# One gated feed-forward block on one core: conditioning rows through TensorE, three weights turned by transfers, and two roots by GpSimd at the start

## The chip, the cores and the metric

The kernel runs on one core of a Trainium2 chip. The time is that of one execution on the device, in microseconds (us). Five engines work side by side, each in the order of its own instruction list: TensorE (PE, with its weight loads as PEld), VectorE (DVE), ScalarE (ACT), GpSimd (POOL) and SyncE (SP), which here does nothing but issue transfers. One SP queue carries nearly all of them; an issue that has to wait holds everything behind it on SP.

## The reference

x has 4 batches of 1024 tokens with 512 features, `up_w` 4096 rows of 512, `down_w` 512 rows of 2048, and `cond` one row of 128 for each batch.

```python
scale = cond @ norm_w.T + 1.0
ms = jnp.mean(x * x, axis=-1, keepdims=True)
h = x * (scale[:, None, :] * jax.lax.rsqrt(ms + EPS))
u = h @ up_w.T
val, gate = jnp.split(u, 2, axis=-1)
h = val * jax.nn.gelu(gate, approximate=False)
hq = h + jax.lax.stop_gradient(act_quant(h) - h)
wq = down_w + jax.lax.stop_gradient(weight_quant(down_w) - down_w)
y = hq @ wq.T
return y + x
```

`act_quant` rounds each token's h to 8 bits by its largest value, `weight_quant` rounds `down_w` to -1, 0 and 1.

## The kernel before

**Tiles.** A batch's up product is cut into 16 slots (j = 0 to 15). Each slot has the 128 gate rows and the 128 value rows of `up_w` that belong together, and gives 128 hidden features for 1024 tokens. Operands are split into a high and a low float16 part, so a product of two tiles has three terms.

**Batch 0** (`plain`, `plain_half`, `plain_first`) multiplies in the plain way: for each slot, each half of 512 tokens and each of gate and value, 12 matmuls of 128x128 by 512 (L917; L960 for the first of all). The order of halves is (0,0), (1,0), (2,0), (0,1), (1,1), (2,1), then (j,0), (j,1) for j from 3 on; the latter are in `first_batch`. Batches 1 to 3 (`slot`, `product`, L902) use a seven-product scheme with sums of weight blocks, and the down product of an earlier batch runs between.

**Weights on the way to TensorE, in batch 0.** `w_load` brings weight j into one of three places (`wn(j)`, by j modulo 3). `w_range` finds its scale. From there two paths lead to the float16 tile `s_tile(j)`, which is one of three buffers, also by j modulo 3:

- for j below `ROWS` (6): `w_scale` on GpSimd (ScalarE for one tile of weight 1), `w_turn` (8 turns on TensorE through PSUM, L646), `w_high` and `w_low` (float16 parts out of PSUM, ScalarE and VectorE), and `w_evac` (a float32 copy `wf(j)` for the sums);
- for j from `ROWS` on: `w_scale` on ScalarE, then `w_rows`: the float16 parts are made untransposed in a staging slot, H[15 + j % 2], and one SP transfer turns them into parts 3 to 6 of `s_tile(j)` (L662). `wf(0)` and `wf(1)` lie in the same two staging slots, 15 and 16.

In both, `s_sums` (GpSimd), `s_high` (ScalarE) and `s_low` (GpSimd) form the sums that the later batches need, in one scratch tile `sf`, and `s_spill` writes the tile to DRAM: one transfer of 896 KB below `ROWS`, three transfers above it, since sums of such a weight are kept unturned. `s_load` brings tiles back in batches 1 to 3, turning the unturned parts on the way. A buffer of `s_tile` can only be filled anew when its products have run and its spill has landed.

**Conditioning.** `cond_first_row` and `cond_scale` make batch 0's scale at the start; `cond_scale_rest` makes the other three in `scT` (128 partitions by 4 blocks by 4 batches). `cond_range`, `cond_spread` and `cond_undo` find powers of two per batch. `cond_rows` writes `scT` for batches 1 to 3 to DRAM as rows (L567: three transfers of 512 pieces of four bytes), in `first_batch(3)`; `cond_load_scale` reads one row back, spread over all partitions (L572, at j = 5 for batch 1), and `cond_bring` scales it on VectorE (L576).

**The start.** x's first four tiles of 128 tokens arrive two by two. ScalarE squares and sums them (L1238), one square root on ScalarE with a refining step on VectorE (`rsqrt_start`) gives all four factors, the tiles are scaled (VectorE, GpSimd and ScalarE), turned on TensorE (`first_turn`, L1262), and turned into float16 (`first_high`, `first_low`, L1266 and L1270). `keep_warm` issues products of zeros. PSUM tiles are handed out in rings by tag: "A" and "E" have two banks, "po" three, "B" one, and the next tile of a tag takes the next bank of its ring, waiting for its last reader.

**Order.** Every call on an engine is recorded as a step by `Plan.add` with an estimated cost. `order` places and replays the steps 40 times with chance variations and emits the best order found, so the program text doesn't fix the order on an engine, except that the first `HEAD` (150) steps, transfers aside, keep program order on their engine. `price` puts four-byte pieces of a transfer at 1.5 KB a microsecond.

Of the kernel before, what the change touches and what calls it, by code (L numbers as in the profile page):

```python
# [114 lines left out]
class Plan:  # L115


    def __init__(self):
        self.steps = []
        self.wrote, self.read = {}, {}  # L120
        self.loaded, self.last = {}, {}
        self.lines = {}

# [4 lines left out]
    def add(self, eng, method, real, args, kwargs):  # L128
# [88 lines left out]
    def place(self, margin, guard):  # L217

        steps = self.steps
        used = {e: Line() for e in ("PE", "ACT", "DVE", "POOL", "SP", "DMA")}
        for s in sorted(steps, key=lambda s: (s.late, s.n)):
            t = max((steps[d].end + lag(steps[d], s) for d in s.deps), default=0.0)
            if s.eng != "PE":
                t += min(margin, max(0.0, s.late - t) * 0.1)
            if s.wait > 0.1:
                t = used["DMA"].put(t + ISSUE, s.wait) - ISSUE
            near = 0.0 if s.eng == "PE" or s.late - t > 1.0 else guard  # L230
            s.start = used[s.eng].put(t - s.before, s.before + s.cost, near) + s.before
            s.end = s.start + (ISSUE + s.wait + LANDING if s.wait else s.cost)
# [39 lines left out]
HEAD = 150  # L272
MARGINS = ((0.3, 0.0), (0.3, 0.15), (0.3, 0.3), (0.25, 0.1))
ROUNDS, MISSES, ISSUE, LANDING, RELOAD = 40, 6, 1.2, 1.5, 6.5
# [106 lines left out]
def glu_quant_kernel(  # L381
# [64 lines left out]
    rows_dram = tc.dram_tile([B, D], F32, name="rows_dram")  # L446
# [105 lines left out]
    def cond_spread(dg, b0, b1, tag):  # L552
        n = b1 - b0
        pd = bank(tag, {"po": 3}.get(tag, 2), [P, B], f"pd_{b0}")[:, :n]
        PE.matmul(pd, ones[:n, :], dg, start=True, stop=True)
        return pd
# [7 lines left out]
    def cond_rows():  # L564

        for b in range(1, B):
            SP.dma_start(out=rows_dram[b].rearrange("(k p) -> p k", p=P), in_=scT[:, :, b])  # L567

    def cond_load_scale(b):

        sc = wpool.tile([P, D], F32, name=f"sc_{b}", tag="sc", bufs=1)
        SP.dma_start(out=sc, in_=rows_dram[b].partition_broadcast(P))  # L572
        return sc
# [55 lines left out]
    ROWS = 6  # L629
# [36 lines left out]
    def w_high(j, ts=(1, 0)):  # L666
        gate, a21, a22 = a_parts(j)
        g, v = (p.rearrange("p (n f) -> p n f", n=2) for p in pw[j])
        if 1 in ts:
            ACT.copy(gate[:, :, 0], g)  # L670
        if 0 in ts:
            ACT.copy(a21[:, 0], v[:, 0])
            ACT.copy(a22[:, 0], v[:, 1])
# [547 lines left out]
    ACT.activation(start_t, one, AF.Sqrt)  # L1221
# [19 lines left out]

    def rsqrt_start(t, y):

        z = sm.tile([P, NA], F32, name="newton", bufs=1)
        ACT.activation(z, t, AF.Sqrt, scale=1.0 / D, bias=eps)
        DVE.tensor_scalar(t, t, 1.0 / D, EPS, ALU.mult, ALU.add)
        DVE.reciprocal(y, z)
        DVE.tensor_tensor(z, y, y, ALU.mult)
        DVE.scalar_tensor_tensor(z, z, -0.5, t, ALU.mult, ALU.mult)
        DVE.scalar_tensor_tensor(y, z, 1.5, y, ALU.add, ALU.mult)  # L1250
# [73 lines left out]
    def second_part():  # L1324
# [6 lines left out]
        ACT.activation(start_t, neghalf[:, 0:1], AF.Gelu)  # L1331


# [22 lines left out]
    def first_batch(j, sc):  # L1356

        if j + 2 <= ROWS:
            w_load(j + 4)
# [5 lines left out]
        rows = ROWS <= n < NJ  # L1365
        if j + 1 < ROWS:
            s_sums(j + 1)
        elif rows:
            s_sums(n)
# [5 lines left out]
        if j + 3 < ROWS:  # L1375
            w_scale(j + 3)
        plain_half(j, 0)
        if j == 3:
            pd = cond_spread(dg, 1, B, "po")
            cond_undo(pd, 1, B)  # L1380
            cond_rows()
# [4 lines left out]
        if j + 1 < ROWS:  # L1386
            s_all(j + 1)
        if n < ROWS:
            w_turn(n)
            w_high(n)  # L1390
            w_evac(n)
            w_low(n)
# [9 lines left out]
        if j + 2 > ROWS and j + 5 < NJ:  # L1402
            w_load(j + 5)
# [3 lines left out]
        if odd:  # L1407
            t.turn()
# [3 lines left out]
        own = rows and j + 1 >= ROWS  # L1412
        if own:
            s_high(n)
            s_low(n, POOL)
        if ROWS <= j + 3 < NJ:
            w_scale(j + 3)
            w_rows(j + 3)
        if own:
            s_spill(n)  # L1420
        elif rows:
            s_sums(n)
            s_all(n)
            w_load(j + 5)
# [59 lines left out]
    w_scale(3)  # L1484
# [18 lines left out]
    w_load(6)  # L1503
# [405 lines left out]
```

## Time and profile before

| | |
|---|---|
| median of 3 runs | 745.95 us (745.18 to 746.45) |
| profiled execution | 745.51 us, of which span 743.7 us |
| TensorE (PE) busy | 725.1 us, 97% of the span |
| VectorE (DVE) busy | 595.4 us, 80% |
| ScalarE (ACT) busy | 405.5 us, 55% |
| GpSimd (POOL) busy | 213.0 us, 29% |
| TensorE's granted clock, mean | 0.995 |
| data moved | 115.74 MB, mean 156 GB/s |

In the views below, times count from the start of the span. A row of the timeline has start, duration, engine, line of the kernel, operation, tile written and tile read, how many instructions were merged, and in brackets how long the engine had been idle and what released it. A row of grouped instructions has their total and mean duration. "PEclk" is the clock that TensorE was granted, as a share of full speed. Matmul ends are modelled, so pace is better read from counts over a stretch than from the mean of one.

### The profile page before, as it was taken

What the parts mean: (1) busy time and instruction counts of PE and PEld (TensorE: products, weight loads), DVE (VectorE), ACT (ScalarE), POOL (GpSimd) and SP (SyncE); (2) the same over time, 40 slices, a digit from 0 to 9 for tenths busy, and PEclk for the clock granted to TensorE, in tenths of its full rate; (3) what the DMA queues carried; (4) which work ended last, traced back from release to release, by engine and by line L of the source; (5) the groups of instructions that cost most, each with busy time, mean ns of one, the idle gap of its engine ahead of it and who ended that gap; (6) DMA issues with size and microseconds to landing.
All of it is one profiled execution on the core that took longest, in us unless ns stands there. A gap on an engine that the chain in (4) does not pass through costs nothing.

```text
span 743.7 us, 10243 instructions
## 1 busy us (share of the span) xinstructions
PE 725.1 (97%) x3684; PEld 362.7 (49%) x3684; DVE 595.4 (80%) x816; ACT 405.5 (55%) x675; POOL 213.0 (29%) x213
## 2 busy tenths in 40 slices
PE   7997899999999999999999999999999999999997
PEld 3553344444444445666444445566444444445743
DVE  6984899869788888877588888878668888855997
ACT  5984687768256677523434767623333666332363
POOL 1575788866640004700004104700000000000010
PEclk9998999999999999999999999999999999999999
DMA  6887788999843465687743455596753444443504
GB/s 240 297 221 98 164 238 192 237 257 247 236 120 99 107 155 115 163 189 178 204 123 100 109 133 145 129 207 147 172 151 106 102 104 100 100 99 100 142 30 170
DMA packets 179567, 115.74 MB, mean 156 GB/s; under 512 B 141750, under 2 KB 147767, under 8 KB 179516
## 3 DMA queue, kind: packets, MB, share of 16 engines
q1 hardware_dynamic: 179226, 114.76, 60.9%
q8 instruction: 29, 0.48, 0.3%
q10 hardware_dynamic: 290, 0.33, 0.1%
q14 instruction: 22, 0.18, 0.1%
HBM read 58.93 MB, written 23.09 MB: 110 GB/s over the span
## 4 chain that ended last, share of the span: by engine, by line
PE 91%; DVE 4%; DMA 3%; ACT 1%; issue 1%; SPq 0%; DVEq 0%; ACTq 0%
PE A L902 33%; PE E L902 17%; PE E L917 10%; PE po L1173 8%; PE B L902 8%; PE A L917 6%; PE B L917 5%; DMA s_dram<-SXY 2%; DVE H L1094 2%; DMA H<-in_x_dram 1%; PE A L1122 1%; PE B L1173 0%; PE po L646 0%; DVE am L1063 0%; PE A L960 0%
## 5 line engine op out<-in xcount | busy, mean ns | idle before, releaser
L902 PEld LDWEIGHTS <-SXY 128*128 128x128 f16 x2016 | 197.3, 98 | 227.9
L902 PE MATMUL A<-R,SXY 128*128 128x512 f16 x1152 | 270.1, 379 | 0.0
L902 PE MATMUL E<-R,SXY 128*128 128x512 f16 x576 | 142.9, 379 | 0.0
L1052 POOL PARTITION_ALL_REDUCE am<-R x8 | 15.6, 1946 | 285.5 <-DVE R L1038 285.5
L1094 DVE TENSOR_TENSOR H<-H,am 128x1024 f32<-128x1024 f32 x64 | 78.1, 1249 | 0.1
L917 PEld LDWEIGHTS <-SXY 128*128 128x128 f16 x462 | 45.4, 98 | 54.5 <-issue 0.8
L902 PE MATMUL B<-R,SXY 128*128 128x512 f16 x288 | 70.8, 379 | 0.0
L1036 DVE TENSOR_REDUCE gm<-H 128x512 f32<-128x1024 f32 x56 | 69.0, 1231 | 0.6
L1000 DVE SCALAR_TENSOR_TENSOR H<-A,sg,t 128x512 f32<-128x512 f32 x48 | 36.0, 749 | 39.0 <-PE A L902 38.3
L988 ACT COPY B<-A 128x512 f32<-128x512 f32 x48 | 27.4, 570 | 67.5 <-PE A L902 66.9
L1173 PE MATMUL po<-wd,R 128*128 128x256 fp8e4 (+1 forms) x448 | 59.1, 275 | 0.0
L980 ACT COPY t<-A 128x512 f32<-128x512 f32 x48 | 28.1, 586 | 56.2 <-PE A L902 56.2
L1013 ACT ACTIVATE t<-t,sg 128x512 f32<-128x512 f32 x48 | 34.6, 722 | 38.3 <-DVE t L1010 38.2
L1173 PEld LDWEIGHTS <-R 128*128 128x128 bf16 (+1 forms) x480 | 47.0, 98 | 15.9
L1016 DVE TENSOR_TENSOR v<-A,v 128x512 f32<-128x512 f32 x48 | 33.2, 691 | 25.2 <-PE A L902 24.0
L997 ACT ACTIVATE t<-B,sg 128x512 f32<-128x512 f32 x48 | 33.0, 687 | 34.2 <-PE B L902 33.7
L1010 DVE TENSOR_TENSOR t<-E,t 128x512 f32<-128x512 f32 x48 | 33.1, 689 | 21.0 <-PE E L902 20.6
L917 PE MATMUL E<-R,SXY 128*128 128x512 f16 x210 | 49.7, 379 | 0.0
L917 PE MATMUL E<-R 128*128 128x512 f16 x162 | 39.9, 385 | 7.7 <-DVE H L945 7.7
L917 PEld LDWEIGHTS <-R 128*128 128x128 f16 x282 | 27.7, 99 | 40.2 <-issue 8.6
L1102 ACT ACTIVATE H<-H 128x1024 f32<-128x1024 f32 x38 | 40.0, 1056 | 8.6 <-DVE H L1094 8.6
L1038 DVE TENSOR_TENSOR R<-R,gm 128x512 f32<-128x512 f32 x56 | 42.9, 765 | 0.9
(234 smaller groups left out, 1040.2 us busy)
## 6 DMA issues: line engine op xcount, KB each, us to landing
SXY<-s_dram SPq DMA_DIRECT2D x66, 256.0 KB, 2.7
SXY<-s_dram SPq DMA_DIRECT2D x18, 384.0 KB, 3.4
H<-in_L_cond_up_w_dram SPq DMA_DIRECT2D x13, 512.0 KB, 4.6
s_dram<-SXY SPq DMA_DIRECT2D x14, 384.0 KB, 5.0
xr<-in_x_dram SPq DMA_DIRECT2D x19, 256.0 KB, 3.0
out_dram<-xr SPq DMA_DIRECT2D x19, 256.0 KB, 2.7
H<-in_x_dram SPq DMA_DIRECT2D x8, 512.0 KB, 4.3
R<-in_L_cond_down_w_dram SPq DMA_DIRECT2D x8, 512.0 KB, 5.5
```

The source lines that it names most:

```text
L902: PE.matmul(o, s[:, w, k, :], tv[:, :, c, l, k, :], start=start and n == 0, stop=stop and n == len(TERMS) - 1, skip_group_check=True,)
L917: PE.matmul(ps, a[k // 2][:, w, k % 2, :], XP[:, l, k, h * TOK : (h + 1) * TOK], start=n == 0, stop=n == len(terms) - 1,)
L997: ACT.activation(cur["t1"], pb, AF.Gelu, scale=gain(g, 1))
L1000: DVE.scalar_tensor_tensor(h_half(g - 1, 0), prev["A"], gain(g - 1, 0), prev["t1"], ALU.mult, ALU.mult)
L1010: DVE.tensor_tensor(prev["t2"], prev["E"], prev["t2"], ALU.add)
L1013: ACT.activation(prev["t2"], prev["t2"], AF.Gelu, scale=gain(g - 1, 1))
L1016: DVE.tensor_tensor(cur["v"], cur["A"], cur["v"], ALU.add)
L1036: DVE.tensor_reduce(gm[0], v, AX.X, ALU.max, apply_absolute_value=True)
L1038: return [largest, lambda: DVE.tensor_tensor(m, m, gm[0], ALU.max)]
L1094: DVE.tensor_tensor(v, v, r.to_broadcast([P, 2, TOK]), ALU.mult)
L1102: ACT.activation(v, v, AF.Copy, bias=MAGIC)
L1173: PE.matmul(po, w[:, j], m, start=start and j == 0, stop=stop and j == n - 1, skip_group_check=True,)
```

## The change

The diff has four parts.

- `cond_rows` turns all of `scT` (16 columns) on TensorE into 16 rows, copies them out of PSUM, and writes them by one transfer of 16 rows of 512 bytes; it now runs right behind `cond_largest(1, B)`. `cond_load_scale` reads a row back as four pieces.
- `ROWS` goes from 6 to 3: weights 3, 4 and 5 take the path of `w_rows`. The calls around slots 0 to 2 and `first_batch` are rearranged to suit; `w_load(6)` and `w_load(7)` move behind the sums of weights 3 and 4, which now read the loaded weight itself.
- At the start, `rsqrt_start` goes. Tiles 0 and 1 get their factors by `rsqrt` (GpSimd's power) as soon as their sums are there, tiles 2 and 3 by a second one; VectorE sums tile 3; scaling and turning go in the order 0, 1, 3, 2, with two warming products between. The product of `cond_spread` takes bank B. The table of Gelu is loaded at the start, and the second table load goes.
- In the planner, steps are tied to program order until `book.tied = False` behind the last `first_turn` of the first four tiles, in place of the first 150; and a step that depends on a transfer is placed up to 4 us (`FERRY`) behind its planned end where there is time.

```diff
+        self.tied = True
...
-            if s.n < HEAD and eng in self.last:
+            if self.tied and eng in self.last:
                 deps.add(self.last[eng])
...
+            for d in s.deps:
+                if steps[d].wait:
+                    t = max(t, steps[d].end + min(FERRY, max(0.0, s.late - steps[d].end - 4.0) * 0.3))
...
-    rows_dram = tc.dram_tile([B, D], F32, name="rows_dram")
+    rows_dram = tc.dram_tile([D // P * B, P], F32, name="rows_dram")
...
     def cond_rows():
-        for b in range(1, B):
-            SP.dma_start(out=rows_dram[b].rearrange("(k p) -> p k", p=P), in_=scT[:, :, b])
+        n = NK * B
+        pr, v = po_bank("pr", [n, P]), H[:n, 8, 0, 64 : 64 + P]
+        PE.transpose(pr, scT.rearrange("p k b -> p (k b)"), ident)
+        DVE.tensor_copy(v, pr)
+        SP.dma_start(out=rows_dram, in_=v)
...
-        SP.dma_start(out=sc, in_=rows_dram[b].partition_broadcast(P))
+        v = rows_dram.rearrange("(k b) p -> b k p", b=B)[b].partition_broadcast(P)
+        SP.dma_start(out=sc.rearrange("q (k p) -> q k p", k=NK), in_=v)
...
-    ROWS = 6
+    ROWS = 3
...
-    ACT.activation(start_t, one, AF.Sqrt)
+    ACT.activation(start_t, one, AF.Gelu)
...
-    for n in range(NA):
-        first_sum(n)
     keep_warm(2)
-    pd = cond_spread(cond_range(pm, 0, 1), 0, 1, "A")
-    keep_warm(7)
-    am = w_largest(0, 1, 2)
-    rsqrt_start(ssq0[:, 0:NA], rs0[:, 0:NA])
-    for n, eng in ((3, DVE), (0, ACT), (2, POOL), (1, ACT)):
-        first_scale(n, eng)
-    w_factor(0, am, 1, 2)
+    pd = cond_spread(cond_range(pm, 0, 1), 0, 1, "B")
+    cond_undo(pd, 0, 1)
+    keep_warm(5)
+    first_sum(0)
+    first_sum(1)
+    rsqrt(ssq0[:, 0:2], rs0[:, 0:2])
+    first_sum(2)
+    first_sum(3, DVE)
+    first_scale(0, ACT)
+    first_scale(1, ACT)
+    rsqrt(ssq0[:, 2:4], rs0[:, 2:4])
+    w_range(0, 1, 2)
+    first_scale(3, DVE)
+    first_scale(2, ACT)
     w_scale(0, (1,))
-    cond_undo(pd, 0, 1)
     ptx = [po_bank(f"ptx_0_{k}") for k in range(3)] + [bank("A", 2, name="ptx_0_3")]
-    for n in (3, 0, 2, 1):
-        first_turn(n, ptx)
+    first_turn(0, ptx)
+    first_turn(1, ptx)
+    keep_warm(2)
+    first_turn(3, ptx)
+    first_turn(2, ptx)
+    book.tied = False
...
-        ACT.activation(start_t, neghalf[:, 0:1], AF.Gelu)
...
     mx = cond_largest(1, B)
+    cond_rows()
     plain_half(0, 1)
     w_range(4)
     w_gain(4)
-    w_scale(4)
+    w_scale(3)
+    w_rows(3)
     s_all(1)
     s_sums(2)
-    w_turn(3)
-    w_high(3)
-    w_evac(3)
-    w_low(3)
...
     plain_half(1, 1)
-    w_load(6)
...
-    w_scale(5)
+    w_scale(4)
+    w_rows(4)
     s_all(2)
     s_sums(3)
+    w_load(6)
...
-    w_turn(4)
-    w_high(4)
-    w_evac(4)
-    w_low(4)
     plain_half(2, 1)
+    w_scale(5)
+    w_rows(5)
     s_all(3)
+    s_sums(4)
+    s_all(4)
+    w_load(7)
```

In `first_batch(j)` the calls for turning on TensorE go, and every j now runs, in this order: sums of weight j + 2, range of j + 3, the first half, `w_load(j + 5)`, the second half, `s_all(j + 2)`, `w_scale(j + 3)` and `w_rows(j + 3)`, for as long as there are such weights.

More of the change, by code (lines that the diff above doesn't have):

```diff
@@ L553, in cond_spread @@
         n = b1 - b0
[L554 removed]
+        pd = bank(tag, {"po": 3, "B": 1}.get(tag, 2), [P, B], f"pd_{b0}")[:, :n]
         PE.matmul(pd, ones[:n, :], dg, start=True, stop=True)
@@ L664, in w_rows, with w_high @@
         )
-    def w_high(j, ts=(1, 0)):
+    def w_high(j, ts=(1, 0), copy=ACT.copy):
         gate, a21, a22 = a_parts(j)
@@ L669, in w_high @@
         if 1 in ts:
-            ACT.copy(gate[:, :, 0], g)
+            copy(gate[:, :, 0], g)
         if 0 in ts:
@@ L1411, in first_batch @@
             d_mean(part)
[L1412 to L1416, printed above, removed]
+        if n < NJ:
+            s_all(n)
+        if j + 3 < NJ:
             w_scale(j + 3)
             w_rows(j + 3)
[L1419 to L1424, printed above, removed]
         for m in D_ROUND[j] if j == D_MEAN else ():
```

32 lines of the change are left out of this document (3 added, 29 removed).

## The prediction

> **What bounds the kernel now.** I began with TensorE, which is busy for 97% of the span, and asked in which stretch the other 3% lie. The table of stretches gives busy time per engine, granted clock, DMA share and GB/s.
>
> ```profile
> span 743.7 us, 10243 instructions
> ```
>
> ```profile
> 60.00:65.00 5.00, 4.76 (x24) 2.31 (x23) 1.20 (x2) 3.74 (x7) 4.51 (x6) 1.00 0.16 38
> 65.00:70.00 5.00, 0.21 (x1) 0.10 (x1) 2.51 (x5) 0.00 (x0) 0.90 (x2) 0.84 1.48 268
> 70.00:75.00 5.00, 4.54 (x15) 2.50 (x14) 1.18 (x3) 0.37 (x1) 0.00 (x0) 0.50 1.01 44
> ...
> 90.00:200.20 110.20, 110.20 (x512) 49.92 (x511) 94.29 (x109) 74.88 (x130) 85.10 (x82) 1.00 0.91 225
> 200.20:743.70 543.50, 538.47 (x2809) 274.54 (x2807) 435.06 (x556) 268.48 (x421) 81.32 (x76) 1.00 0.52 133
> ```
>
> From 90 us on TensorE is the bound. Between 65 and 70 us it does nothing, and in the 5 us behind that it runs at half clock. The DMA engines are over 100% busy there and then move only 44 GB/s: many small packets. The list of TensorE's waits names the releaser.
>
> ```profile
> PE E L917 <- DVE H L945: 7.7, 2, 5.0
> ```
>
> VectorE is not the cause, though; it was waiting itself. The timeline gives start, duration, engine and line:
>
> ```profile
> 50.27 0.46 SPq L567 DMA_DIRECT2D rows_dram<-scT  x1
> ...
> 61.80 0.34 SPq L572 DMA_DIRECT2D sc<-rows_dram  x1
> ...
> 62.67 1.52 SPq L567 DMA_DIRECT2D rows_dram<-scT  x2
> ...
> 64.30 1.68 SPq L714 DMA_DIRECT2D s_dram<-SXY  x1
> ...
> 67.46 0.49 DVE L576 TENSOR_SCALAR sc<-sc,ux 128x512 f32<-128x512 f32 x1 [6.26 <-DMA sc<-rows_dram]
> ...
> 69.00 0.74 DVE L945 SCALAR_TENSOR_TENSOR H<-E,sg,t 128x512 f32<-128x512 f32 x1
> ```
>
> The SP queue's waits and the chain of waits complete it:
>
> ```profile
> SPq L572 <- DMA rows_dram<-scT: 9.5, 1, 9.5
> ```
>
> ```profile
> 64.30 17.26 DMA s_dram<-SXY
> ```
>
> The 2 KB row of batch 1, written in pieces of four bytes (L567), has not landed 9.5 us after SP turns to the load that reads it. SP issues nothing meanwhile. Then VectorE stands 6.26 us before L576, with TensorE's evacuation (L945) queued behind it: that is the 5.0 us stop. The other two rows go out at 62.67, and the spill behind them takes 17.26 us; it lands at 81.6, holds a weight buffer till then, and a second stop of 2.7 us (7.7 less 5.0) follows.
>
> **The change, part by part.** (1) *The rows as 16 rows of 512 bytes.* What the stall costs I count in matmuls, by line L917 alone (busy time and count in TensorE's column) and, in the second fence, by the weights' turns (L646):
>
> ```profile
> 60.00:90.00 30.00, 19.95 (x85) 8.64 (x84) 0.89 0.82 156
> 90.00:200.20 110.20, 110.16 (x511) 49.72 (x509) 1.00 0.91 225
> ```
>
> ```profile
> 30.00:60.00 30.00, 2.40 (x16) 2.00 (x16) 1.00 0.79 213
> 60.00:90.00 30.00, 2.18 (x8) 1.71 (x8) 0.89 0.82 156
> ```
>
> ```profile
> 31.11 0.49 PE L1262 MATMUL po<-ident,H 128*128 128x128 f32 x3
> ...
> 32.86 2.75 PE L917 MATMUL E<-R 128*128 128x512 f16 x12
> ```
>
> A matmul takes 110.16/511 = 0.2156 us at full clock, and the 16 turns from 31.11 to 32.86 took 1.75, 0.109 each. The work between 60 and 90 us is then 85 x 0.2156 + 8 x 0.109 = 19.2 of 30 us. 0.1 us went on two small products, so stops and the low clock behind them cost 10.7 us. All of it has its origin in the row writes, and I take **-10.7** for it. Bounds: not below -10.7; at the other end nothing, if another transfer holds the engines. Whether the others could keep up without the stop: VectorE, the fullest of them, has 94.29 us of work in the 110.2 us behind it (86%) and had 1.20 + 2.51 + 1.18 = 4.9 us in the 15 us above, so it has room.
>
> What is put in its place, and moved ahead from slot 3 to just behind the conditioning's products: one turn, one copy of 16 partitions, one SP issue, instead of three issues. On SP it goes past the loads of weights 6 and 7 and the spills of slots 1 and 2, which now wait up to one issue (0.46 us) behind it, and longer if the copy is late. TensorE has one small product more ahead of half (0,1). Its nearest row for landing is another small write:
>
> ```profile
> SPq L1077 <- DMA am_dram<-am: 1.5, 2, 0.8
> ```
>
> A reader of 4 KB waited 0.8 us at most for its writer. Lower bound nothing, upper bound 9.5 us as today; I take the lower row, because its pieces are long too. A load of a row is now in four pieces for each partition; VectorE needs it only some 20 us after the write can have landed, and that covers it. Cost 0; with the cover gone, at most the 6.3 us of L576.
>
> (2) *Weights 3 to 5 by transfers.* The 24 turns go: 24 x 0.109 = **-2.6** on TensorE, which is full there. GpSimd loses its scalings. The rest:
>
> ```profile
> L636 ACT ACTIVATE H<-H,iv 128x512 f32<-128x512 f32 x21 | 13.9, 713 | 7.0 <-DVE iv L619 7.0
> ...
> L661 DVE TENSOR_TENSOR H<-H 128x1024 f16<-128x1024 f32 x10 | 14.7, 1472 | 1.7 <-ACT H L660 1.7
> ...
> L660 ACT CAST H<-H 128x1024 f16<-128x1024 f32 x10 | 10.4, 1045 | 0.5 <-POOL H L697 0.3
> ...
> L686 ACT COPY H<-po 128x512 f32<-128x512 f32 x10 | 5.9, 590 | 0.3 <-DVE SXY L679 0.2
> ...
> L670 ACT CAST SXY<-po 128x512 f16<-128x512 f32 x3 | 1.7, 577 | 0.0
> ```
>
> ```profile
> L662 SPq DMA_TRANSPOSE SXY<-H x7: 1935/2304/3119, 82.1 to 177.9; - x7
> ...
> DMA to landing us min/median/max: 4.3/4.8/5.1
> ```
>
> ```profile
> 40.09 0.72 POOL L695 TENSOR_TENSOR H<-H 128x256 f32<-128x256 f32 x1
> ...
> 52.85 2.75 PE L917 MATMUL B<-R,SXY 128*128 128x512 f16 x12
> ```
>
> ScalarE gains 2 x 0.713 + 1.045 = 2.5 us a weight and loses two copies (1.2), a cast (0.58) and two casts of half the size (0.29 to 0.58 each): 2.3 to 2.9. VectorE swaps three subtractions over 1,024 elements for one (1.47). So both stay where they are. New is a wait: weight 3's float16 copy goes to the staging slot that the sums of weight 1 read until 40.81 (L695). From there copy 1.05, subtraction 1.47, and 4.8 from issue to landing make 48.1; 50.4 if the 2.3 us of issuing come on top. Slot 3 starts at 52.85, less the 16 turns (1.75) 51.1. The cover is thus 0.7 to 3.0 us, thin. Behind the waiting transfer SP holds weight 6's load, due much later. With longest issue and landing and one more pass of ScalarE and VectorE (2.5) it would land at 54.0: 2.9 late, some 4 with the slow clock that followed the old stop. Bounds 0 to +4; I take **+1.0**, since the middle of the estimate is in time. Slots 4 and 5 come 10 and 21 us later. In batches 1 to 3 these three weights' reloads turn too, with 18 issues more on SP; after 200.2 us the DMA share is 0.52 and each tile is fetched a slot (some 9 us) ahead, so 0.
>
> A page of the Trainium skill speaks against this part: VectorE: DVE Perf Modes, "The three transpose paths" and the rules behind it, says to turn 128x128 blocks on TensorE where PSUM will do, and gives 390 ns there against 1309 ns by transfer. A weight has 16 such blocks in float16, so by that page alone an estimate is 20.9 us for a weight, slot 3 would start 43.3 + 20.9 - 51.1 = 13.1 us late, and the sum would be 744.6 (732.5 - 1.0 + 13.1). The trace has 4.8 us for just this transfer; the sum goes by the trace, and that extreme gets 0.01 of the chance of late weights below.
>
> (3) *The start.*
>
> ```profile
> 8.56 0.63 ACT L1238 ACTIVATE R<-H 128x512 f32<-128x512 f32 x1 [0.84 <-DMA H<-in_x_dram]
> ...
> 11.13 1.34 ACT L1255 ACTIVATE H<-H,rs 128x512 f32<-128x512 f32 x2 [0.91 <-DVE rs L1250]
> ...
> 13.91 0.69 ACT L1266 ACTIVATE R<-po,scT 128x512 f16<-128x512 f32 x1 [1.43 <-DVE sw L616]
> ...
> 15.31 0.39 PE L960 MATMUL B<-R,SXY 128*128 128x512 f16 x1 [0.68 <-ACT SXY L670]
> ...
> 18.04 0.60 PE L960 MATMUL A<-R 128*128 128x512 f16 x2
> ...
> 20.52 0.74 DVE L1270 SCALAR_TENSOR_TENSOR R<-A,scT,R 128x512 f16<-128x512 f32 x1
> ...
> 27.81 1.06 POOL L807 TENSOR_TENSOR rs<-ssq,neghalf 128x4 f32<-128x4 f32 x1 [0.84 <-DVE ssq L806]
> ```
>
> ```profile
> 65.07 0.19 POOL L806 TENSOR_SCALAR ssq<-ssq 128x2 f32<-128x2 f32 x1 [0.40 <-ACT xt L836]
> 65.34 0.71 POOL L807 TENSOR_TENSOR rs<-ssq,neghalf 128x2 f32<-128x2 f32 x1
> ```
>
> A root of two tiles takes GpSimd 66.05 - 65.07 = 1.0 us. The first can run while ScalarE squares tile 2 (8.56 to 9.2). ScalarE then scales tiles 0 and 1 (1.34) till about 10.7, when the second root is ready (squares done about 9.5, plus 1.0 and hops); tile 2 follows till 11.4, tile 3 on VectorE beside it. Turning a tile takes 4 x 0.109 = 0.44 us, and with two warming products (2 x 0.216) between, the last ends about 12.4; the first float16 of x starts at 12.4 where it started at 13.91: **-1.5**. Bounds: 0, if the products are fed no sooner, to -2.5. One thing is lost. Counting the tiles of tag A, the value product's bank used to be the other one than that of x's fourth turn; it is now the same, so the first value product must follow its last reader (L1270, 20.52 to 21.26) and not precede it as at 18.04. In today's order that would be 3.2 us; VectorE's steps there are no longer tied to program order, so it can come forward. I take **+0.4** of 0 to 3.2. ScalarE's second table load goes, in a stretch where TensorE runs anyway: 0.
>
> The planner's new spacing behind transfers changes orders everywhere; behind 200 us TensorE loses nothing that it could give back, so 0 within 0.7 either way.
>
> Sum: the profiled execution took 745.51 us, of which 743.7 are span. 745.51 - 10.7 - 2.6 + 1.0 - 1.5 + 0.4 = 732.1. The median of the runs shown is 745.95, 0.44 more: **732.5**.
>
> **The rivals.** *Weights late at slots 3 to 5.* The thin cover speaks for it, the 4.8 us landing under a full queue against it. The price is 4 in place of 1.0 at slot 3 and half as much at a later slot: 732.5 + 3 + 2 = 737.5.
>
> *The stall has another cause*, the transfers of that stretch as such. For it: spills of whole weights go out among them. Against it: 44 GB/s at full busy time. Only the rest is gained: 732.5 + 10.7 = 743.2.
>
> *GpSimd's first power is slow.* The first root in the kernel, at 27.81, took 1.06 us for four columns and shows no start-up beyond it; should one hide in the idle start, it delays every first tile; where it eats the whole gain of 1.5, the time is 734.0. The Trainium skill, GPSIMD Engine Reference, "Instruction dispatch", gives about 6 us for the first call to freshly loaded code; by that an estimate is 732.5 + 6 = 738.5, and no start-up of that size shows at 27.81.
>
> *Slower: each weight just too late.* Place: the ring of three weight buffers. Thirteen weights, not ten, pass spill, transfer and products in it, on one SP queue. If TensorE stops at each of slots 3 to 15 for 1.2 us, 15.6 us are lost, and 732.1 - 1.0 + 15.6 + 0.4 = 747.1. It decides once a stop at every slot exceeds 1.1 us. Against it: with ten the ring held TensorE full for 110.2 us.
>
> **How the numbers follow.** A measurement of this kernel tells 0.2% (1.5 us) from nothing. My forecast has 0.68, with its own range 728.5 to 736 (732.5 less 1.0 for a start of -2.5, 1.4 for no cost of bank and slot and 0.7 of order is 729.4, rounded down for the runs' own spread; 3.5 of the unknown costs on the other side). Late weights 0.14, another cause 0.06, slow power 0.03, slower 0.06, and 0.03 remain for no change. Faster: 0.68 + 0.14 + 0.06 + 0.03 = 0.91; same 0.03; slower 0.06. The range takes in the late weights with some clock loss more: 728.5 to 741.
>
> **What would show it.** The table of stretches between 60 and 90 us should have TensorE at 30.0 and the clock at 1.00; no wait of SP on the rows above 3 us, and spills landing in some 5 us there. TensorE's first product with float16 of x at about 13.8; the first value product behind L1270's last. No turn of weights behind 30 us. A TensorE wait for weight 3 near 50 us of over 2 us makes me too low; a stop near 65 us that remains makes the first part wrong.

## The result and the profile after

| | before | after |
|---|---|---|
| median | 745.77 us (4 runs, 745.18 to 746.45) | 737.66 us (4 runs, 736.02 to 740.12) |
| ratio of the two | | 0.9894 (0.9863 to 0.9924) |
| profiled execution | 745.51 us, span 743.7 | 740.12 us, span 738.3 |
| batch 1's first product | 199.99 us | 187.57 us |
| from there to the end of the span | 543.7 us | 550.7 us |

The change takes 8.1 us off, 1.1%; on the two chips of the experiments where both kernels ran it is 7.6 us each time. The result is 5.2 us above the forecast of 732.5, within the range, but above the 736 that the forecast case gave itself. The last two rows hold the finding: TensorE begins batch 1 12.4 us earlier, and 7.0 us of it are given back behind that point. The span and busy time of each engine from the page:

```profile
span 738.3 us, 10181 instructions
...
PE 724.8 (98%) x3661; PEld 361.1 (49%) x3661; DVE 592.2 (80%) x808; ACT 404.4 (55%) x665; POOL 209.8 (28%) x210
```

TensorE's busy time has hardly changed (725.1 us before). The table of stretches of the changed kernel, with the columns of before: the first three rows are where the old stall was, then come the start and the turn from batch 0 to batch 1 ("the turn" below, where no weight or tile is named).

```profile
60.00:65.00 5.00, 5.00 (x25) 2.26 (x24) 2.85 (x5) 4.41 (x11) 1.58 (x3) 1.00 0.86 186
65.00:70.00 5.00, 5.00 (x25) 2.29 (x24) 2.40 (x7) 4.36 (x8) 2.52 (x3) 1.00 0.96 314
70.00:75.00 5.00, 5.00 (x25) 2.29 (x24) 4.48 (x5) 3.85 (x9) 4.40 (x4) 1.00 0.67 179
11.00:16.00 5.00, 4.99 (x26) 4.13 (x25) 3.30 (x7) 2.27 (x5) 1.28 (x2) 0.66 0.43 158
200.00:204.00 4.00, 0.91 (x5) 0.20 (x2) 3.93 (x5) 0.80 (x2) 0.00 (x0) 0.89 0.67 231
204.00:212.00 8.00, 7.65 (x24) 3.01 (x25) 4.85 (x8) 0.95 (x2) 0.00 (x0) 0.63 0.12 33
```

From 60 to 75 us TensorE is full at full clock, and the DMA engines move 314 and then 179 GB/s from 65 us on, where it was 268 and then 44. Between 200 and 204 us it now works 0.91 us, with a low clock behind that (0.63). In the kernel before it was full in both of these stretches, and at full clock in the start:

```profile
11.00:16.00 5.00, 3.12 (x22) 2.27 (x22) 3.27 (x14) 3.36 (x6) 2.26 (x3) 1.00 0.74 281
...
200.00:204.00 4.00, 4.00 (x20) 1.86 (x19) 3.68 (x7) 0.71 (x2) 2.64 (x3) 1.00 0.97 326
204.00:212.00 8.00, 8.00 (x39) 3.62 (x37) 6.89 (x10) 4.13 (x9) 1.75 (x1) 1.00 0.59 182
```

TensorE's waits in the changed kernel name the releasers:

```profile
PE po L1180 <- DVE R L1105: 3.4, 1, 3.4
PE po L1259 <- ACT H L1252: 2.4, 1, 2.4
```

The first is the stop at 200 us. The second stands in the start; the kernel before stops at the same place for 2.8 us, for a step of VectorE (L483). There is no wait for a DMA. The timeline of the changed kernel at the turn:

```profile
185.71 1.65 POOL L717 TENSOR_TENSOR R<-H,R 128x256 f16<-128x256 f32 x1
...
187.57 1.46 PE L909 MATMUL A<-R,SXY 128*128 128x512 f16 x6
...
195.40 0.38 POOL L1052 PARTITION_ALL_REDUCE ready<-ready  x1 [8.04 <-issue]
195.70 3.86 POOL L1059 PARTITION_ALL_REDUCE am<-R  x2
...
197.61 1.27 DVE L1064 TENSOR_SCALAR am<-am 128x512 f32<-128x512 f32 x1 [4.31 <-POOL am L1059]
...
198.92 3.39 DVE L1070 RECIPROCAL am<-am 128x128 f32<-128x128 f32 x4
...
202.34 1.22 DVE L1101 TENSOR_TENSOR H<-H,am 128x1024 f32<-128x1024 f32 x1
203.60 0.69 DVE L1105 TENSOR_SCALAR R<-H 128x1024 bf16<-128x1024 f32 x1
204.21 0.68 DVE L1023 TENSOR_TENSOR v<-A,v 128x512 f32<-128x512 f32 x1
...
204.35 0.82 PE L1180 MATMUL po<-wd,R 128*128 128x512 fp8e4 x2 [3.44 <-DVE R L1105]
```

And the same place in the kernel before:

```profile
193.30 1.65 POOL L710 TENSOR_TENSOR R<-H,R 128x256 f16<-128x256 f32 x1
...
199.99 1.46 PE L902 MATMUL A<-R,SXY 128*128 128x512 f16 x6
...
201.29 0.57 POOL L1045 PARTITION_ALL_REDUCE ready<-ready  x1 [6.34 <-issue]
...
203.69 0.43 DVE L1057 TENSOR_SCALAR am<-am 128x512 f32<-128x512 f32 x1
...
207.60 0.69 DVE L1016 TENSOR_TENSOR v<-A,v 128x512 f32<-128x512 f32 x1 [0.87 <-PE A L902]
```

When batch 0's last weight sums are done, GpSimd goes over to its reduction over partitions (the largest value of each token), and the profile shows an empty stretch ("issue", that is, no wait it knows of) before it: 6.34 us before the change, 8.04 after. I call it the change-over; the planner's price for it is 6.5 us (`RELOAD`). Before the change the last sum ended at 194.95, 5.0 us ahead of batch 1. Now it ends at 187.36, only 0.2 us ahead: TensorE came forward by 12.4 us and GpSimd by 7.6. VectorE's order has the token scale (L1064, four times L1070, L1101, L1105: 1.27 + 3.39 + 1.22 + 0.69 = 6.6 us) ahead of the evacuation of batch 1's PSUM (L1023, L1017), which reads a bank out so that TensorE can write it again. So VectorE waits 4.31 us for GpSimd and then works off the scale, and TensorE stops, by name at a down product put forward (L1180) that needs L1105; the evacuation comes only at 204.21, 16.6 us behind batch 1's first product, where it was 7.6 before.

The start of the changed kernel:

```profile
7.01 1.25 PE L1275 MATMUL A<-H 128*128 128x512 f16 x5
...
9.11 0.74 POOL L814 TENSOR_TENSOR rs<-ssq,neghalf 128x2 f32<-128x2 f32 x1
...
9.88 1.95 ACT L1252 ACTIVATE H<-H,rs 128x512 f32<-128x512 f32 x3 [1.38 <-POOL rs L814]
...
10.65 0.55 PE L1259 MATMUL po<-ident,H 128*128 128x128 f32 x3 [2.39 <-ACT H L1252]
...
14.56 0.69 ACT L1263 ACTIVATE R<-po,scT 128x512 f16<-128x512 f32 x1 [2.73 <-PE po L1259]
...
15.78 0.39 PE L967 MATMUL B<-R,SXY 128*128 128x512 f16 x1
```

The first turn is issued at 10.65, but the clock falls to half from about 12 us on, x's turns last past 14.5, and the first product comes at 15.78 (15.31 before, 13.8 forecast).

### The profile page after: what moved, and what is told of

Same layout as the page of the kernel before. It is cut to its first block, busy times and chain, and to the rows that moved or that the text cites. A ratio compares the mean times of both kernels' runs of the same rounds, so it can differ in the third digit from the quotient of the medians.

```text
span 738.3 us, 10181 instructions
## 1 busy us (share of the span) xinstructions
PE 724.8 (98%) x3661; PEld 361.1 (49%) x3661; DVE 592.2 (80%) x808; ACT 404.4 (55%) x665; POOL 209.8 (28%) x210
## 4 chain that ended last, share of the span: by engine, by line
PE 85%; DVE 7%; issue 2%; POOL 2%; ACT 2%; DMA 1%; SPq 0%; DVEq 0%; POOLq 0%; ACTq 0%
PE A L909 33%; PE E L909 16%; PE E L924 8%; PE po L1180 8%; PE B L909 8%; PE A L924 5%; PE B L924 4%; DVE H L1101 2%; DVE am L1070 1%; DMA H<-in_x_dram 1%; PE A L1129 1%; POOL R L717 1%; PE B L1180 0%; DVE gm L1043 0%; DVE SXY L1220 0%
## 5 line engine op out<-in xcount | busy, mean ns | idle before, releaser
L909 PEld LDWEIGHTS <-SXY 128*128 128x128 f16 x2016 | 198.0, 98 | 230.6 <-issue 4.8
L909 PE MATMUL E<-R,SXY 128*128 128x512 f16 x576 | 143.8, 379 | 0.0
L1059 POOL PARTITION_ALL_REDUCE am<-R x8 | 17.8, 2239 | 266.0 <-DVE R L1045 266.0
L1101 DVE TENSOR_TENSOR H<-H,am 128x1024 f32<-128x1024 f32 x64 | 79.7, 1271 | 0.1
L924 PEld LDWEIGHTS <-SXY 128*128 128x128 f16 x486 | 47.5, 98 | 56.7 <-issue 0.2
L1180 PE MATMUL po<-wd,R 128*128 128x256 fp8e4 (+1 forms) x448 | 59.8, 276 | 3.4 <-DVE R L1105 3.4
L1180 PEld LDWEIGHTS <-R 128*128 128x128 bf16 (+1 forms) x480 | 46.9, 98 | 19.5 <-DVE R L1105 3.9
L924 PE MATMUL E<-R,SXY 128*128 128x512 f16 x234 | 54.3, 379 | 0.0
L1017 DVE TENSOR_TENSOR t<-E,t 128x512 f32<-128x512 f32 x48 | 33.0, 688 | 23.4 <-PE E L909 22.9
L1023 DVE TENSOR_TENSOR v<-A,v 128x512 f32<-128x512 f32 x48 | 33.1, 690 | 22.0 <-PE A L909 20.5
L999 ACT COPY v<-E 128x512 f32<-128x512 f32 x48 | 28.1, 586 | 33.1 <-PE E L909 27.3
L813 POOL TENSOR_SCALAR ssq<-ssq 128x2 f32<-128x2 f32 x14 | 4.2, 300 | 139.1 <-ACT H L843 98.5
L1045 DVE TENSOR_TENSOR R<-R,gm 128x512 f32<-128x512 f32 x56 | 41.1, 735 | 1.0
```

The lines of the kernel that those rows point to most:

```text
L909: PE.matmul(o, s[:, w, k, :], tv[:, :, c, l, k, :], start=start and n == 0, stop=stop and n == len(TERMS) - 1, skip_group_check=True,)
L924: PE.matmul(ps, a[k // 2][:, w, k % 2, :], XP[:, l, k, h * TOK : (h + 1) * TOK], start=n == 0, stop=n == len(terms) - 1,)
L1017: DVE.tensor_tensor(prev["t2"], prev["E"], prev["t2"], ALU.add)
L1023: DVE.tensor_tensor(cur["v"], cur["A"], cur["v"], ALU.add)
L1045: return [largest, lambda: DVE.tensor_tensor(m, m, gm[0], ALU.max)]
L1101: DVE.tensor_tensor(v, v, r.to_broadcast([P, 2, TOK]), ALU.mult)
```

## The experiments

They ran on three chips, and each group is compared with the kernel before on its own chip: 741.77 us (20 runs, 739.32 to 746.47), 743.87 (11 runs, 738.98 to 746.6) and 745.34 (11 runs, 741.75 to 748.81). The changed kernel itself was not run on the first of these chips. Where a kernel keeps an order found before, only what is issued at the named steps differs; with a changed price the order is searched anew. Added lines shift the line numbers.

**Is it the down product put forward that stops TensorE at the turn?** The emitted order of the changed kernel, but with the six down products of batch 0 behind the products they had been moved past (slot 9, where the text has them).

```diff
+    h0 = len(book.steps)
     pair.first([po_bank(f"po_{b}_{a}_{n}") for n in range(3)])
+    if b == 1 and a == 0:
+        book.held += range(h0, len(book.steps))
...
-    book.emit(book.order())
+    book.emit(book.hold(book.order()))
```

> The changed kernel in its own order, with the first down products of batch 1 (6 matmuls that the order had put forward, the first at 204.35 us) back behind slot 9's products. Theory: that matmul waits 3.4 us for its quantised tile and the low clock behind it costs some 2.6 more; without it TensorE is full and at clock 1.00 between 200 and 210 us, the profiled execution loses up to 6 us and the median 2 to 4 (734 to 735.7), and the runs lie closer together than the 4.1 us of the changed kernel. Rival: slot 0 of batch 1 stops at the same place for its own operands, the stop only changes its name, and the median stays within 1 us of 737.7.

737.67 us (9 runs, 735.02 to 740.21), ratio 0.9949 (0.9928 to 0.9969). Its stretch at the turn:

```profile
200.00:204.00 4.00, 1.73 (x8) 0.68 (x7) 3.93 (x6) 1.40 (x3) 0.00 (x0) 1.00 0.82 256
```

and the first of TensorE's waits:

```profile
PE A L926 <- DVE v L1040: 2.8, 1, 2.8
```

The stop stays and gets another name: now a product of batch 1 (L926) waits for the evacuation (L1040) that stands behind the token scale on VectorE. So the rival holds, and the down product was not the cause.

**Is it too little warming that slows the start?** The emitted order of the changed kernel, the five products of zeros issued three times each.

```diff
+    w0 = len(book.steps)
     keep_warm(5)
+    book.times.update(dict.fromkeys(range(w0, len(book.steps)), 3))
```

> The changed kernel in its own order, with the five warming products ahead of the first turns issued three times over (15). Theory: the start lost its gain because TensorE stood from 8.3 to 10.7 us and then had half the clock from 11.9 to 15.2; kept busy it has clock 1.00 there, the first product with float16 of x comes at about 14.1 in place of 15.8, and the median falls by 1.7 us (to 736). Rival: the start is paced by the scaling of x's tiles or by VectorE's weight steps and not by the clock; the first product stays at 15.5 or later and the median within 0.7 us of 737.7.

736.2 us (6 runs, 735.26 to 738.49), ratio 0.9932 (0.9914 to 0.9949). Its start:

```profile
11.00:16.00 5.00, 4.53 (x31) 2.89 (x30) 4.41 (x9) 3.45 (x7) 1.21 (x2) 1.00 0.50 187
```

The clock stays at 1.00, the first product comes at 14.53 in place of 15.78 and batch 1 at 186.29 in place of 187.57: 1.3 us. Against the kernel with the late down products on the same chip the median is 1.5 us lower. The fifteen products end at 10.54, where x's first turn starts at 10.59, so the idle 2.4 us are gone too: this run doesn't tell the number of products from the closed gap. The turn is as bad as before (TensorE waits 2.6 us for the token scale).

**What of the old stall was the four-byte pieces, and what the load waiting behind them?** The emitted order of the changed kernel, with three transfers of four-byte pieces at the new place, and the row read back from there. What is issued in place of the changed kernel's write and load:

```diff
+    for b in range(1, B):
+        nc.sync.dma_start(out=old_dram[b].rearrange("(k p) -> p k", p=P), in_=scT[:, :, b])
...
+    nc.sync.dma_start(out=sc, in_=old_dram[b].partition_broadcast(P))
```

> The changed kernel in its own order, with the three rows written in four-byte pieces again, at the new place (43 us), and read back from there. Theory: such a row holds the transfer queue some 10 us, three of them 30; weight 3's turned transfer behind them lands past 70 us instead of 50, so TensorE stops at slot 3 for about 20 us and the time is 750 to 765. Rival: the rows cost only through the load that waits for them; that load is now 40 us later, so the time stays within 2 us of 737.7.

738.88 us (10 runs, 736.56 to 741.68), ratio 0.9958 (0.9937 to 0.9978): far less than I expected of the pieces, and within the 2 us of the rival. TensorE's wait, the SP queue and a stretch:

```profile
PE B L952 <- DMA SXY<-H: 2.0, 1, 2.0
```

```profile
37.69 2.57 SPq L596 DMA_DIRECT2D old_dram<-scT  x3
40.31 0.75 SPq L863 DMA_DIRECT2D xn<-in_x_dram  x1
46.08 5.87 SPq L697 DMA_TRANSPOSE SXY<-H  x1
```

```profile
45.00:50.00 5.00, 5.00 (x25) 2.25 (x23) 4.25 (x10) 4.66 (x8) 3.16 (x4) 1.00 1.02 70
```

The pieces still fill the DMA engines (70 GB/s at 1.02), they take 12.7 us from issue to landing (the second of the three, the only one whose landing the profile gives; the 16 rows of the next kernel took 1.4), and the transfer of weight 3 behind them needs 5.87 us to issue and makes slot 3 2.0 us late. Batch 1 starts at 191.84, 3.7 us behind the 188.17 of the kernel with the late down products. That is a third of the old 10.7 (and 1.7 of it comes back at the turn, where this profile has a shorter change-over). What is missing from the old stall here is the load: it came 11.5 us behind the write (50.27 and 61.80) and held SP and then VectorE, while in this kernel it is issued at 88.64, long after the pieces have landed. So some two thirds may have hung on that wait; this is by elimination, in another order and with the write 12.6 us earlier, and no run had four-byte pieces without the early load in the order of before.

**The rows alone.** The order of the kernel before, in which only the row writes and their reading back are changed: one turn on TensorE, one copy, one transfer of 16 rows, loads in four pieces. Weights 3 to 5, the start and the planner stay. The planner still places the steps of the lines with -, and those with + are issued in their place:

```diff
-            SP.dma_start(out=rows_dram[b].rearrange("(k p) -> p k", p=P), in_=scT[:, :, b])
+            nc.tensor.transpose(pr, scT.rearrange("p k b -> p (k b)"), ident)
+            nc.vector.tensor_copy(v, pr)
+            nc.sync.dma_start(out=new_dram, in_=v)
...
-        SP.dma_start(out=sc, in_=rows_dram[b].partition_broadcast(P))
+        v = new_dram.rearrange("(k b) p -> b k p", b=B)[b].partition_broadcast(P)
+        nc.sync.dma_start(out=sc.rearrange("q (k p) -> q k p", k=NK), in_=v)
```

> The kernel before in its own order, with the rows turned on TensorE and written as 16 rows of 512 bytes by one transfer, and read back in four pieces; nothing else. Theory: the stop of 65 to 70 us and the low clock behind it go, 10.7 us of the 745.8: 735. Rival A: other transfers make the stop, the time stays above 743. Rival B: only the first stop goes and the second, at 84 to 87 us, stays: 738 to 740.

737.11 us (4 runs, 735.81 to 737.5), ratio 0.9937 (0.992 to 0.9955), about as much as the others of this group. The SP queue and the two stretches of the old stall:

```profile
52.22 0.34 SPq L592 DMA_DIRECT2D new_dram<-H  x1
52.61 0.42 SPq L861 DMA_DIRECT2D am<-in_x_dram  x1
53.64 0.37 SPq L603 DMA_DIRECT2D sc<-new_dram  x1
```

```profile
60.00:65.00 5.00, 4.58 (x24) 2.25 (x22) 4.86 (x9) 3.75 (x7) 4.35 (x7) 1.00 0.44 179
65.00:70.00 5.00, 4.54 (x25) 2.44 (x25) 2.89 (x6) 2.88 (x5) 0.87 (x1) 1.00 0.25 90
```

The load follows its write by 1.4 us, and TensorE keeps 9.1 us of the 10 (28.2 of the 30 from 60 to 90 us). In its profile batch 1 starts at 190.98, GpSimd's last sum ended at 185.95, 5.0 us ahead as in the kernel before, and nothing stops at the turn.

Run again on the third chip, beside the changed kernel:

> The kernel before in its own order with only the rows turned and written as 16 rows, beside the whole change on one chip. Theory: the rows carry nearly all that the change gains, since the turns saved on TensorE (2.6) are given back at the turn of the batches; median within 1 us of the control. Rival: the other parts still add up to 2 us or more; the control is lower by that.

> The changed kernel as the control of this chip. Both theories: median 736 to 738.

737.29 us (6 runs, 735.82 to 740.78), ratio 0.9899 (0.987 to 0.9929), against 737.77 (6 runs, 735.17 to 740.67), ratio 0.9900 (0.9868 to 0.9932), for the whole change. Within the noise the rows alone are worth as much as the whole change; what the other parts gain up to batch 1's first product (187.43 us against 191.16 in the two profiles) is lost again behind it (549.6 us to the end against 544.4). This second profile of the rows alone has a change-over of 7.72 us (6.39 in the first), VectorE waits 1.71 for it (0 in the first), and TensorE stops 1.2: the same order, another length.

**Is it the planner's price for the change-over?** If so, an order searched with a higher one should not stop.

```diff
-ROUNDS, MISSES, ISSUE, LANDING, RELOAD, FERRY = 40, 6, 1.2, 1.5, 6.5, 4.0
+ROUNDS, MISSES, ISSUE, LANDING, RELOAD, FERRY = 40, 6, 1.2, 1.5, 10.0, 4.0
```

> The changed kernel with one number of the planner changed: GpSimd's change-over to the reduction is taken as 10 us in place of 6.5, and the order is searched anew. Theory: the stop at the turn of the batches comes from VectorE's chain for the tokens' scale (L1064 to L1105, 6.6 us), which the order puts ahead of slot 0's evacuation and which then waits 2.4 to 4.3 us for GpSimd; with the evacuations ahead of it TensorE is full between 200 and 212 us and the median is 3 to 5 us under the control's (732.5 to 734.5). Rival: GpSimd's lateness itself stops batch 1 wherever VectorE's chain stands, since the quantised tiles are due; the stop moves behind 212 us and the median stays within 1 us of the control.

> The changed kernel once more, as the control for the two that follow on the same chip. Both theories: batch 1's first product at 187 to 188 us, GpSimd's first reduction 7 to 8 us behind it, TensorE stopped or slowed between 200 and 212 us, median 736.5 to 738.5.

> The kernel before once more, for a profile on this chip, where it has been between 739.3 and 746.5. Theory: SP waits 9 to 10 us for the four-byte row in every execution, but how long VectorE and then TensorE stand behind it changes, so the stop of 5.0 us is there and of another length. Rival: the stop is missing in the shorter executions.

734.37 us (5 runs, 733.59 to 735.34), ratio 0.9878 (0.9843 to 0.9912); the changed kernel beside it 736.29 (6 runs, 735.95 to 737.85), ratio 0.9909 (0.9874 to 0.9944). At the turn, with the price raised:

```profile
200.00:204.00 4.00, 4.00 (x20) 1.79 (x19) 2.80 (x4) 2.27 (x4) 0.00 (x0) 1.00 0.61 174
204.00:212.00 8.00, 8.00 (x38) 3.63 (x37) 2.47 (x4) 2.61 (x5) 3.95 (x3) 1.00 0.71 212
```

The stop is gone, though the reduction comes as late as 204.51: the scale now stands behind the evacuations on VectorE. The new price also made a new search, so this run by itself doesn't show that the price did it. The gain is 1.9 us and not the 3 to 5 expected, as this order's profile has the slowest start of all (first product at 17.25, clock 0.50 from 11 to 16) and batch 1 only at 190.22. The changed kernel beside it kept full clock at the start in its profile (first product 14.40, batch 1 at 186.16), had a change-over of 6.64 and lost 4.6 at the turn, so that its batch 1, its reduction (6.4 us behind) and its median all came somewhat earlier than expected; the profile of the kernel before (744.92 us) had three stops behind its rows where the first had two, 7.7 us in sum again, behind a wait of SP of 8.6 us.

**Both mended.** The higher price and the tripled warming together, first with 10.0, then on the third chip with 9.0.

> The same with the five warming products issued three times over (15). Theory: the two faults are apart and their gains add; first product at 14.5 in place of 15.8 to 16.4 us, batch 1 begins 1.3 to 1.9 us earlier, and the median is 1.2 to 1.9 us under the kernel without them (731 to 733). Rival: what the start gains is given back at the turn, as GpSimd's last sums set that, and the median stays within 0.5 us of the kernel without them.

733.42 us (5 runs, 733.01 to 733.94), ratio 0.9863 (0.9829 to 0.9898); first product at 14.99. That is 0.95 us under the kernel without the warming, less than the 1.2 expected at least.

> The changed kernel with 15 warming products and GpSimd's change-over taken as 9 us in place of 6.5. Theory: like the kernel with 10 us and 15 warming products (733.4), with TensorE full from 200 to 212 us; 732.5 to 734.5. Rival: at 9 us VectorE's chain stands close behind the first evacuations and still holds the next ones, so a stop of 1 to 3 us stays; 735 to 736.5.

731.9 us (6 runs, 731.56 to 732.12), ratio 0.9822 (0.9798 to 0.9847). This beats both kernels: 13.4 us under the one before and 5.9 under the changed one on the same chip, and its runs lie within 0.6 us where those of the changed kernel spread over 5.5. The turn, in stretches and on VectorE:

```profile
200.00:204.00 4.00, 4.00 (x20) 1.86 (x19) 3.29 (x6) 0.97 (x2) 0.00 (x0) 1.00 0.68 234
204.00:212.00 8.00, 8.00 (x39) 3.72 (x38) 6.31 (x9) 4.45 (x10) 0.94 (x2) 1.00 0.52 136
```

```profile
194.25 0.69 DVE L1040 TENSOR_TENSOR v<-A,v 128x512 f32<-128x512 f32 x1 [1.57 <-PE A L926]
194.86 0.68 DVE L1034 TENSOR_TENSOR t<-E,t 128x512 f32<-128x512 f32 x1
195.46 0.57 DVE L1081 TENSOR_SCALAR am<-am 128x512 f32<-128x512 f32 x1
```

The evacuation (L1040, L1034) now goes ahead of the scale (L1081), which finds GpSimd's result there. From batch 1's first product (186.64) to the end it takes 543.6 us, what it took before the change.

**The old start.** The changed kernel with the start of the kernel before (one root for four tiles, nine warming products, the old order of tiles), searched anew.

```diff
-    rsqrt(ssq0[:, 0:2], rs0[:, 0:2])
...
+    keep_warm(7)
+    am = w_largest(0, 1, 2)
+    rsqrt_start(ssq0[:, 0:NA], rs0[:, 0:NA])
...
-    first_turn(0, ptx)
-    first_turn(1, ptx)
-    keep_warm(2)
-    first_turn(3, ptx)
-    first_turn(2, ptx)
+    for n in (3, 0, 2, 1):
+        first_turn(n, ptx)
```

> The changed kernel with the start of before (one square root on ScalarE and VectorE's refining, seven warming products, tiles turned in the order 3, 0, 2, 1, second table load), order searched anew. Theory: the first product comes at 14.9 to 15.3 us in every execution, at full clock, where the new start gives 14.4 with the clock kept and 15.8 to 17.3 without; so the start by itself is worth from -0.5 to +2 us and nothing on average. VectorE's chain at the turn has one evacuation further forward in this order, so that stop is shorter: median 734.5 to 737. Rival: the new start's gain of 1.5 us is real in most executions, and this kernel is slower than the control by 1 us or more.

734.17 us (6 runs, 731.82 to 735.54), ratio 0.9851 (0.9824 to 0.9879): 3.6 under the changed kernel, more than expected. First product at 15.28 with full clock, batch 1 at 186.66. But the new order also has GpSimd done with its sums by 181.2, 5.5 us ahead of batch 1, and a VectorE wait of only 0.66 at the turn, so this run doesn't tell the start from the order; it shows that the new start isn't needed for a time below the changed kernel's. It also shows that the higher price isn't needed to lose the stop: with the planner's 6.5 TensorE works 8.93 of the 9 us from 195 to 204.

The profiles of all kernels with the order of the changed one or of the kernel before, by the length of the change-over, in us:

| kernel | change-over | VectorE waits | batch 1's first product | from there to the end |
|---|---|---|---|---|
| before | 6.34 | 0 | 199.99 | 543.7 |
| before, second | 6.40 | 0 | 200.00 | 543.1 |
| rows alone | 6.39 | 0 | 190.98 | 542.9 |
| rows alone, second | 7.72 | 1.71 | 191.16 | 544.4 |
| changed, four-byte pieces | 6.14 | 2.40 | 191.84 | 547.7 |
| changed, second | 6.64 | 2.90 | 186.16 | 548.3 |
| changed, late down products | 7.00 | 3.26 | 188.17 | 549.4 |
| changed, third | 7.17 | 3.43 | 187.43 | 549.6 |
| changed, more warming | 7.17 | 3.43 | 186.29 | 550.1 |
| changed | 8.04 | 4.31 | 187.57 | 550.7 |

In the six with the changed kernel's order VectorE's wait is the change-over less 3.73 or 3.74 us each time. With the planner's own 6.5 it would still wait 2.8, so a low price for the change-over is not the whole of it; what else in its estimates let it choose this order was not looked into.

## Why the prediction was right, and where it was wrong

*The rows (-10.7): the mechanism right, the size nearly.* In the changed kernel TensorE is full at full clock from 60 to 90 us, and no load waits for the rows to land. In the order of before, the rows alone bring batch 1's first product forward by 9.0 us (199.99 to 190.98); 1.8 us of stops stay between 60 and 90 us. In the medians they bring 4.7 us on the first chip (741.77 to 737.11) and 8.1 on the third (745.34 to 737.29). The kernel before ran from 738.98 to 748.81 us, so a sum that starts from one execution of 745.51 takes that execution's stall for every one's; no profile of a short execution shows how its stall differs. The four-byte run suggests that the larger part of the stall hung on the load that waited.

One sign that the prediction gave went against it: SP does wait over 3 us at the rows, not for their landing but ahead of the write, for VectorE's copy of the turned rows.

```profile
SPq L573 <- DVE H L572: 6.1, 1, 6.1
```

The prediction had named this ("longer if the copy is late") without a price. It cost nothing here: weight 3's turn, issued next but one, waited another 1.4 us for its own operand (L668), and TensorE has no wait for a transfer.

*Weights 3 to 5 (-2.6) and slot 3 (+1.0).* The turns are gone (the last is at 26.8 us), and there is no wait for weight 3, so the +1.0 was 0; the -2.6 was not measured by itself. The transfers themselves:

```profile
45.52 2.07 SPq L669 DMA_TRANSPOSE SXY<-H  x1
...
52.68 2.55 PE L924 MATMUL B<-R,SXY 128*128 128x512 f16 x11
```

From 45.52 this turn took 5.3 us to land (others of its kind in this profile from 4.3), so it was there at 50.8, 1.9 us ahead of slot 3. The cover held, thin as it was. The figure of 1309 ns a block that the prediction quoted from the Trainium skill (VectorE: DVE Perf Modes, "The three transpose paths") gives 20.9 us by the prediction's estimate of 16 times that; 16 blocks in one transfer took 5.3, and the measurement decides. The rival of late weights falls, and with it the slower one of a stop at every slot.

*The shared PSUM bank (+0.4): 0.* The first value product follows the bank's last reader directly (18.31 behind 18.26), as forecast, but TensorE had other products until then, and its waits show none for that reader.

*GpSimd's power: no start-up.* It takes 0.74 us at 9.11, so that rival falls. The Trainium skill, GPSIMD Engine Reference, "Instruction dispatch", gives about 6 us for the first call to freshly loaded code. The change-over to the reduction is of that order (8.04 at 195 us), but the trace shows it again at the later returns to the reduction (5.83 at 318.01, 6.14 at 501.24), and not at the power. What GpSimd does in it no run here shows.

*The start (-1.5): wrong, by 2.0, and outside its bounds: the first product came 0.5 us later than before.* The step that failed is the pace: "Turning a tile takes 4 x 0.109 = 0.44 us". TensorE has had only five warming products, idles 2.4 us, and is then granted half clock from about 12 to 15 us. Where the clock stays full, the first product comes at 14.4 (the same kernel, second profile) to 15.0 (with more warming); so some 1.4 of the 2.0 us are the clock, and what is left has two likely sources: ScalarE's scaling starts at 9.88, 0.5 behind the forecast (10.7 - 1.34), and four turns of a weight (L653, 0.44 us at full clock) stand between x's. Batch 1 began at 187.57 where the sum says 199.99 - 10.7 - 2.6 + 1.0 - 1.5 + 0.4 = 186.6; the 2.0 of the start less the 1.4 that slot and bank didn't cost account for 0.6 of the 1.0 between them.

*"Behind 200 us TensorE loses nothing that it could give back, so 0 within 0.7": the step that made the miss.* It looked at TensorE alone and took GpSimd, VectorE and the planner's order for followers of it. They aren't: GpSimd's end came forward by 7.6 us against TensorE's 12.4, and VectorE came to stand waiting for its 6 to 8 us of change-over, covered before, ahead of an evacuation. It cost 7.0, 4.6 and 5.9 us in the three profiles of the changed kernel. That the place of the scale in VectorE's order is the cause is shown from three sides: without the down product the stop stays; the same order costs more the longer the change-over is; and the three kernels whose orders put the scale behind the evacuation lose nothing (543.3 to 543.6 us from batch 1's first product to the end), with the reduction at 191.63 as at 204.51.

Together, for the profiled execution: the forecast span was 743.7 - 13.4 = 730.3; 7.0 at the turn and 1.0 ahead of it give the 738.3 measured. The kernel with both faults mended takes 731.9, close to the 732.5 forecast for the change itself, though on a chip of its own and in an order of its own.

That the result lies in the range of 728.5 to 741 is luck in part. Its upper 5 us were there for late weights, whose price of 737.5 is almost the time measured, and no weight came late; the loss sits in the term that was put at 0.

The stall's going did not by itself take GpSimd's lead. In all four profiles with the order of before, with the stall or without, the last sum ends 5.0 us ahead of batch 1; in all six with the order of the changed kernel it is 0.2, with a slow start or a fast one. So the lead was lost with the other parts of the change and the order found for them. Which of these took it is not settled; no run told weights 3 to 5 and the planner's spacing from the search.

## What to carry to other kernels

When a change moves the bound engine forward and the order is searched anew, ask for every engine whether it comes forward by as much, and look at the next place where they meet: cover that one of them had in the old order may be gone there. A value that is needed late should stand in an engine's order behind work that the bound engine needs now; where a planner decides that, compare its price for a long idle step (6.5 us here) with the longest in the profiles (8.04). A small strided write can be dear through what waits for it on a queue, so check who stands behind the reader before counting the bytes.

## What the runs showed of the hardware

GpSimd's change-over from tensor operations to the reduction over partitions took 6.04 to 8.04 us at the turn to batch 1 in 14 profiles, and for one emitted order it varied from 6.64 to 8.04 between executions on three chips; with DMA shares of 1.00 and 1.01 over 187 to 195 us it was 8.04 in one kernel and 6.10 in another, so that share doesn't explain it.

The granted clock at the start depends on more than the idle time. The kernel before idles 2.8 us (8.9 to 11.7) behind a last group of seven warming products and kept 1.00 from 11 to 16 us, as did the four other profiles with its start; the changed one idles 2.4 us behind a group of five and lost the full clock in five of six profiles with its start (0.50 to 0.77 over that stretch). Those five idle 2.07 to 2.74 us, the one that kept it 1.70. With a group of fifteen it kept 1.00 in all three, but these idle 0.4 us at most, so no run here tells the number of products from the gap.

512 pieces of four bytes, the second of three such transfers issued together, took 12.7 us to land where 16 rows of 512 bytes, with more data, took 1.4; the transfers issued meanwhile were held back with them (5.87 us for the issue of a weight's turn, which takes about 2 in the changed kernel).
